# A router in four column groups: weights held still, tokens streamed, and the logits turned back

## The chip, the cores and the metric

The kernel runs on one core of a Trainium2 chip. The metric is the device time of one execution in microseconds (us); runs of the same kernel are given as a median with lowest and highest. The profile names the engines of the core: PE is TensorE (matrix products, PEld its weight loads), DVE is VectorE, ACT is ScalarE, POOL is GpSimd, SP is SyncE, which issues most DMA transfers. Each engine executes its own queue in order and waits on semaphores for the others.

## The reference

One macaron block: half a feed-forward step, attention, half a feed-forward step. Each takes a layer norm of x and is added to x. X is 16 x 256 x 256 float32, so 4096 tokens of 256 features. Cut to what matters here:

```python
# feed-forward (twice, with the same weights)
x = w_norm * xf * rsqrt(mean(xf * xf) + EPS)
logits = x @ w_router                       # 256 -> 32 experts
probs = softmax(logits)
w_topk, sel = top_k(probs, 4)               # each expert takes up to 128 tokens
y = (silu(buf @ w_gate) * (buf @ w_up)) @ w_down        # 32 experts, 176 wide
out = scatter of y, weighted with w_topk
sh = silu(x @ sw_gate) * (x @ sw_up) @ sw_down          # shared expert, 704 wide
out = out + sigmoid(x @ w_shared_gate) * sh             # the shared gate: one column
return inp + out
# attention: 16 heads, 8 key/value heads of 32, rope, tanh soft cap, causal softmax
```

All products of the kernel are in float32.

## The kernel before

The 4096 tokens are 32 tiles of 128, in eight groups (`g`) of four tiles. The x tile stays on chip for the whole kernel.

*Routing.* `route(n, g)` is a generator that makes the router of group g in feed-forward n (0 or 1). It emits a stretch of instructions and yields, and its caller emits other work between the stretches; the number that it yields is not used by the caller. Its stretches: moments (L220, L221) and roots; `xr`, the normalised tokens (L248); two halves of four transposes `pt` (L257), each turned into `xnT` by ScalarE (L260), with the update of x (L268) between; then the router. Eight matmuls write `pl` (L276): the stationary operand is a 128x128 piece of `xnT` (128 features by 128 tokens), the moving one is `wr`, 33 columns wide (32 experts and the shared gate), and two pieces of 128 features add up. VectorE copies `pl` to `lg` (L280), takes the gate column (L281), the maximum (L283) and the difference (L285). After the next yield come exp on ScalarE (L287) and the tail: sum, reciprocal, probabilities `pr` (L290 to L297), a copy of them into `xr` on POOL (L298), the write of `xr` to the table `xtab` in device memory (L299), the four largest of each token (L303 to L306) and `mask` (L307).

*Experts.* `slots` counts the mask with `pc` (L323), in four column groups of 32, and makes the lists of tokens `idx`; `expert` gathers 128 tokens (L413), turns them (`pte`, L429; `xgT`, L432), multiplies (`pge`, L437; `poe`, L450), scales the product to `y` (L452) and adds it to the sums `acc` in device memory with a scatter (L453). The 32 experts are pipelined three deep.

*The shared expert* is the filling. `shared(pool, g)` yields after each piece: five pieces of four matmuls `pg` (L390) and one of two, then four of six matmuls `po` (L402), whose result VectorE adds to x (L406). `Fill.take(us)` emits pieces until their named costs add up to `us`; what is taken too much is kept in `left` and makes the next take smaller. The pieces of group g may be taken when `ready` is above g.

*Order.* The order on TensorE is that of the program everywhere (`manual_schedule`), on VectorE, ScalarE and POOL in the attention only; elsewhere a planner with its own costs sets it. `feed_forward` calls route, slots and expert with takes between (the constants on top: ROUTE_FILL, MASK_FILL, EXPERT_FILL). The routing of groups 0 to 6 of the second feed-forward is spread over the attention's loop over `units`: a group's `route` starts in step j=1 of its turn and ends two turns later. In that loop `project` makes queries, keys and values (`pq` L503, `pv` L531), `scores` makes `sc` (L552) with tanh and exp on ScalarE, and `values` makes `den` and `y` (L598) in four column groups. When no group is left to project (`mine` is None, the last turns), those pieces are absent.

*Buffers.* The pool `ps1` has two PSUM buffers of the kind "mm", which `pt`, `pl`, `po`, `pc`, `pte`, `pq` and `pv` take in turn: a tile waits until the one before the last has been read.

*The end.* After the last scatter SP reads `acc` back in eight pieces; POOL (L465, and L745 for single tiles) and VectorE (L745) add them to x, and the groups are stored. Groups whose filling was finished when the experts ended are added and stored whole.

Of the kernel before, what the change touches and what calls it, by code (L numbers as in the profile page):

```python
# [22 lines left out]
GT = 4  # L23
# [17 lines left out]

ROUTE_FILL, SLOT_FILL, FIRST_FILL, EXPERT_FILL, SUM_FILL, PROJECT_FILL = 3.0, 1.7, 6.0, 2.4, 17.0, 1.5
LAST_FILL = 8.0
MASK_FILL, ROW_FILL = 4.0, 3.2
WARM = (9, 3)
AHEAD = 3
SPARE = (1.0, 0.0, 3.0, 4.0)
PROJECT_PIECES = ((2, 1), (0, 2), (2, 1), (0, 0))  # L50


_COLS = {}
_n = 0
for _name, _w in [("ident", P), ("cos", T), ("sin", T), ("triu", P), ("iota", CAP),
                  ("ustrict", P), ("last", P), ("block", P // NT), ("slot", 1), ("spare", 1), ("base", 1)]:
    _COLS[_name] = (_n, _w)
    _n += _w
# [3 lines left out]
def _constants():  # L62
    k = np.zeros((P, NCONST), np.float32)

    def put(name, value):
        o, w = _COLS[name]
        k[: value.shape[0], o : o + w] = value

    put("ident", np.eye(P))
    inv = (1.0 / np.float32(10000.0) ** (np.arange(0, HD, 2).astype(np.float32) / np.float32(HD))).astype(np.float32)  # L70
    freqs = np.arange(T, dtype=np.float32)[:, None] * inv[None, :]
    emb = np.concatenate([freqs, freqs], -1)
    put("cos", np.tile(np.cos(emb).T, (P // HD, 1)))

    sign = np.where(np.arange(HD) < HD // 2, -1.0, 1.0)
    put("sin", np.tile(np.sin(emb).T * sign[:, None], (P // HD, 1)))
    put("triu", np.triu(np.ones((P, P))))

    put("iota", np.tile(np.arange(CAP) + 0.5, (P, 1)))

    p = np.arange(P)[:, None]
    blocks = np.kron(np.eye(P // NT), np.ones((NT, NT)))
    put("ustrict", blocks * np.triu(np.ones((P, P)), 1))
    put("last", np.tile(p % NT == NT - 1, (1, P)))
    put("block", p // NT == np.arange(P // NT))
    put("slot", p + 0.5)
    put("spare", p + NTOK - P)
    put("base", p % NT * P)
    return k
# [3 lines left out]
def macaron_kernel(ctx: ExitStack, tc: tile.TileContext, X, Wq, Wk, Wv, Wo, w_norm, w_router, w_gate, w_up,  # L93
# [26 lines left out]
    def const(name, parts=P):  # L120
        o, w = _COLS[name]
        return kc[:parts, o : o + w]
# [8 lines left out]
    nc.gpsimd.memset(power, -0.5)  # L131
    wnorm = cpool.tile([P, 2], F32, name="wnorm")
    nc.sync.dma_start(wnorm, w_norm.rearrange("(c p) -> p c", p=P))
    wr = cpool.tile([P, 2, E + 1], F32, name="wr")
    nc.sync.dma_start(wr[:, :, 0:E], w_router.rearrange("(c p) e -> p c e", p=P))
    nc.sync.dma_start(wr[:, :, E : E + 1], w_shared_gate.rearrange("(c p) e -> p c e", p=P))


    sw = cpool.tile([P, 2, 2 * FS], F32, name="sw")
# [12 lines left out]
        load_x(g)  # L152
    nc.sync.dma_start(kc[:, P:], consts[:, P:])
    triu = cpool.tile([P, P], BF16, name="triu")
    nc.vector.tensor_copy(triu, const("triu"))

    wq = cpool.tile([P, 2, 2, 2, P], F32, name="wq")
    wk = cpool.tile([P, 2, C], F32, name="wk")
# [72 lines left out]
    def route(n, g):  # L231


        mv = moments(g)


        s2 = root("s2", mv, 1.0 + RMS_EPS, RMS_EPS * LN_EPS)
        s1 = root("s1", mv, 1.0, LN_EPS)
        xa = stat.tile([P, GT], F32, name="xa", bufs=5)
        nc.gpsimd.tensor_scalar(xa, s1, 0.5, 1.0, ALU.mult, ALU.add)  # L240
        xb = stat.tile([P, GT], F32, name="xb", bufs=5)
        nc.gpsimd.tensor_mul(xb, s1, mv[:, :, 0])
        nc.gpsimd.tensor_scalar_mul(xb, xb, -0.5)
        yield 0.0
        xr = rows.tile([P, GT, XW], F32, name="xr")
        for t in range(GT):
            i = g * GT + t
            nc.vector.tensor_scalar(  # L248
                xr[:, t, 0:C], x[:, i, :], mv[:, t, 0:1], s2[:, t : t + 1], ALU.subtract, ALU.mult
            )  # L250
        yield 0.0
        for h in range(GT // 2):
            pt = ps1.tile([P, 2, 2, P], F32, tag="mm", name="pt")
            for j in range(2):
                t = 2 * h + j
                for c in range(2):
                    nc.tensor.transpose(pt[:, c, j, :], xr[:, t, c * P : (c + 1) * P], ident)  # L257
            i0 = (g * GT + 2 * h) * P
            for c in range(2):
                nc.scalar.activation(  # L260
                    xnT[:, c, i0 : i0 + 2 * P], pt[:, c].rearrange("p j t -> p (j t)"), AF.Identity,
                    scale=wnorm[:, c : c + 1],
                )
            yield 0.5
            if h == 0:
                for t in range(GT):
                    i = g * GT + t
                    nc.scalar.activation(  # L268
                        x[:, i, :], x[:, i, :], AF.Identity, bias=xb[:, t : t + 1], scale=xa[:, t : t + 1]
                    )  # L270
                yield 0.0
        pl = ps1.tile([P, GT, E + 1], F32, tag="mm", name="pl")
        for t in range(GT):
            i = g * GT + t
            for c in range(2):
                nc.tensor.matmul(  # L276
                    pl[:, t, :], lhsT=xnT[:, c, i * P : (i + 1) * P], rhs=wr[:, c, :], start=(c == 0), stop=(c == 1)
                )
        lg = stat.tile([P, GT, E + 1], F32, name="lg", bufs=2)
        nc.vector.tensor_copy(lg, pl)  # L280
        nc.vector.tensor_copy(gate[:, g * GT : (g + 1) * GT], lg[:, :, E])  # L281
        mx = stat.tile([P, GT, 1], F32, name="mx")
        nc.vector.tensor_reduce(mx[:, :, 0], lg[:, :, 0:E], AX.X, ALU.max)  # L283
        ex = stat.tile([P, GT, E], F32, name="ex", bufs=2)
        nc.vector.tensor_sub(ex, lg[:, :, 0:E], mx.to_broadcast([P, GT, E]))  # L285
        yield 1.9
        nc.scalar.activation(ex, ex, AF.Exp)  # L287
        yield 0.0
        tot = stat.tile([P, GT, 1], F32, name="tot")
        nc.vector.tensor_reduce(tot[:, :, 0], ex, AX.X, ALU.add)  # L290
        nc.vector.reciprocal(tot, tot)

        pr = stat.tile([P, GT, E + 4], F32, name="pr", bufs=1)
        nc.vector.memset(pr[:, :, E : E + 4], -1.0)
        nc.vector.tensor_mul(ex, ex, tot.to_broadcast([P, GT, E]))

        nc.vector.scalar_tensor_tensor(pr[:, :, 0:E], ex, TINY, ex, ALU.is_ge, ALU.mult)  # L297
        nc.gpsimd.tensor_copy(xr[:, :, C:XW], pr[:, :, 0:E])  # L298
        nc.sync.dma_start(xtab[n][g * GW : (g + 1) * GW, :].rearrange("(t p) c -> p t c", p=P), xr)  # L299
        top = stat.tile([P, GT, 8], F32, name="top")  # L300
        hit = stat.tile([P, GT, E + 4], F32, name="hit", bufs=1)
        for t in range(GT):
            nc.vector.max(top[:, t, :], pr[:, t, 0:E])  # L303
        nc.vector.memset(top[:, :, TOPK:8], -1.0)
        for t in range(GT):
            nc.vector.match_replace(hit[:, t, :], top[:, t, :], pr[:, t, :], 2.0)  # L306
        nc.vector.tensor_single_scalar(  # L307
            mask[:, :, g * GT : (g + 1) * GT], hit[:, :, 0:E].rearrange("p t e -> p e t"), 1.5, ALU.is_gt
        )
        yield 0.0  # L310
# [61 lines left out]

    def shared(pool, g, last):

        sg = stat.tile([P, GT], F32, name="sg")
        nc.scalar.activation(sg, gate[:, g * GT : (g + 1) * GT], AF.Tanh, scale=0.5)
        nc.vector.tensor_scalar(sg, sg, 1.0, 0.125, ALU.add, ALU.mult)
        act = pool.tile([P, len(FC), GW], F32, name="act")
        cols = slice(g * GW, (g + 1) * GW)
        for k, (f0, fw) in enumerate(FC):  # L380
            pg = big.tile([P, 2, GW], F32, tag="big", name="pg")
            if fw == P:
                at = [f0, FC[-1][0] + f0]
                b = pg[:, 1, :]
            else:
                at = [2 * f0]
                b = pg[fw : 2 * fw, 0, :]
            for s, w0 in enumerate(at):
                for c in range(2):
                    nc.tensor.matmul(  # L390
                        pg[:, s, :], lhsT=sw[:, c, w0 : w0 + P], rhs=xnT[:, c, cols], start=(c == 0), stop=(c == 1)
                    )
            si = act[:fw, k, :]
            nc.scalar.activation(act[:, k, :], pg[:, 0, :], AF.Tanh, scale=0.5)  # L394
            nc.vector.scalar_tensor_tensor(si, si, 1.0, pg[:fw, 0, :], ALU.add, ALU.mult)  # L395
            nc.vector.tensor_mul(si, si, b)  # L396
            yield 1.7 * len(at)
# [260 lines left out]
    def feed_forward(n, pool, works, fill):  # L658


        for g, work in works.items():
# [7 lines left out]
            if n == 0 and g == 0:  # L669
                warm(WARM[1])  # L670
            fill.take(ROUTE_FILL)
            advance(work, 2)
            advance(later[2])
            fill.ready = g + 1
            fill.take(ROUTE_FILL)
            next(work)
        if n == 0:
# [74 lines left out]
    with tc.tile_pool(name="attn", bufs=1, reuse_waits="tile") as pool:  # L752
# [5 lines left out]
        for k in range(len(units) + 2):  # L758
# [37 lines left out]

            if j == 3:
                advance(routing.get(g - 1))
            spare_time(SPARE[j])
            if j == 3:  # L800
                advance(routing.get(g - 2))
# [63 lines left out]
```

## Time and profile before

| | us |
|---|---|
| median of 3 runs (lowest to highest) | 1070.91 (1069.13 to 1072.49) |
| the profiled execution: its time | 1070.05 |
| the profiled execution: its span | 1068.3 |
| TensorE busy in the span | 1031.8 |
| first route stage | 0 to 114 |
| slots and experts of the first feed-forward | 114 to 339 |
| attention, with the routing of groups 0 to 6 | 397 to 780 |
| slots and experts of the second feed-forward | 800 to 1038 |

The span is that of the instructions; the time of the execution has 1.7 us around it. A row of a group gives its line, engine, operation, the tiles (out<-in), shapes and count, then busy us and the mean ns of one, then the idle time of the engine before it and what ended that. A row of a timeline gives start, length and the same names, with the wait in brackets. A row of stages gives for each stretch the busy us of each engine, the clock that TensorE was granted (1.00 is full), the share of the DMA engines and GB/s. A matmul's length is its latency; several overlap, so their cost is read from the distance between starts.

### The profile page before, as it was taken

Reading aid. Unit: us, or ns where it says so; the run is one execution under the profiler, and the core shown is the slowest. Engines: PE = TensorE matmul, PEld = TensorE weight load, DVE = VectorE, ACT = ScalarE, POOL = GpSimd, SP = SyncE. Lnnn points to the kernel's source line nnn. Section 1 sums busy time; section 2 is a strip of 40 time slices with the busy share of each in tenths; the row PEclk is TensorE's granted clock in tenths of the full one; section 3 lists DMA queues with packets and bytes.
Section 4 is the critical chain, followed back from the end, with each engine's and each line's share of the span. In section 5 each row is a group of like instructions: output and inputs, shape, how many; then the busy total and the mean of one; then the engine's idle time right before and its main releaser. Section 6 shows DMA issues by size and latency. Waiting matters only on the chain.

```text
span 1068.3 us, 15597 instructions
## 1 busy us (share of the span) xinstructions
PE 1031.8 (97%) x5432; PEld 650.7 (61%) x5432; DVE 628.8 (59%) x1681; ACT 399.9 (37%) x761; POOL 499.3 (47%) x552
## 2 busy tenths in 40 slices
PE   9999999999999899999999999998999999999998
PEld 5657656777767544545455556554466567767675
DVE  5755664445343457777778777774556744443434
ACT  3343111222221246675658475756621112221210
POOL 4500102555542298788476767562311024545536
PEclk9999999999999999999999999999999999999999
DMA  9811701778773000000101010000030027777739
GB/s 297 243 69 45 233 12 48 170 159 172 168 164 58 30 21 1 20 21 2 42 1 42 2 43 1 23 1 23 25 82 23 6 56 157 163 153 170 167 55 314
DMA packets 137869, 92.97 MB, mean 87 GB/s; under 512 B 80512, under 2 KB 135104, under 8 KB 137792
## 3 DMA queue, kind: packets, MB, share of 16 engines
q1 hardware_dynamic: 125504, 74.16, 24.9%
q0 software_dynamic: 12288, 17.83, 9.7%
q8 instruction: 43, 0.70, 0.3%
q14 instruction: 34, 0.28, 0.1%
HBM read 60.99 MB, written 30.97 MB: 86 GB/s over the span
## 4 chain that ended last, share of the span: by engine, by line
PE 89%; DVE 6%; ACT 3%; issue 1%; DMA 0%; SPq 0%; POOL 0%; ACTq 0%; POOLq 0%
PE pg L390 28%; PE po L402 14%; PE pge L437 8%; PE pq L503 8%; PE poa L616 5%; PE poe L450 5%; PE sc L552 5%; PE y L598 3%; PE den L598 3%; PE pv L531 3%; PE pl L276 2%; PE pte L429 1%; PE pt L257 1%; DVE act L395 1%; DVE act L396 1%
## 5 line engine op out<-in xcount | busy, mean ns | idle before, releaser
L390 PE MATMUL pg<-xnT,sw 128*128 128x512 f32 x704 | 320.7, 600 | 1.8 <-ACT p L559 1.8
L390 PEld LDWEIGHTS pg<-xnT,sw 128*128 128x128 f32 x704 | 131.1, 192 | 138.8 <-issue 130.7
L453 POOL DMA_INDIRECT acc<-y,idx x64 | 101.4, 1584 | 183.6 <-DVE y L452 104.8
L402 PE MATMUL po<-swd,act 128*128 128x256 f32 x768 | 179.9, 383 | 6.6 <-DVE act L396 2.4
L402 PEld LDWEIGHTS po<-swd,act 128*128 128x128 f32 x768 | 143.0, 190 | 35.7 <-issue 13.0
L395 DVE SCALAR_TENSOR_TENSOR act<-act,pg 128x512 f32<-128x512 f32 x96 | 65.7, 684 | 167.9 <-ACT act L394 167.8
L394 ACT ACTIVATE act<-pg 128x512 f32<-128x512 f32 x96 | 57.2, 596 | 271.3 <-PE pg L390 271.3
L559 ACT ACTIVATE p<-sc 128x512 f32<-128x512 f32 (+1 forms) x128 | 97.4, 808 | 106.8 <-PE sc L552 106.3
L564 POOL TENSOR_SCALAR_AFFINE_SELECT p<-p 128x512 f32<-128x512 f32 x128 | 82.3, 667 | 48.1 <-ACT p L562 45.7
L413 POOL DMA_INDIRECT xg<-xtab,idx x64 | 67.9, 1061 | 76.8 <-DVE idx L368 57.9
L437 PE MATMUL pge<-xgT,wgu 128*112 128x128 f32 (+1 forms) x768 | 95.8, 275 | 5.9 <-issue 4.4
L562 ACT ACTIVATE p<-p 128x512 f32<-128x512 f32 (+1 forms) x128 | 100.9, 844 | 0.0
L437 PEld LDWEIGHTS pge<-xgT,wgu 128*112 128x112 f32 (+1 forms) x768 | 88.8, 182 | 8.7 <-issue 7.6
L552 PE MATMUL sc<-qT,kT 32*128 32x256 f32 (+1 forms) x512 | 68.5, 535 | 4.7 <-DVE act L396 3.4
L406 DVE SCALAR_TENSOR_TENSOR x<-po,sg,x 128x256 f32<-128x256 f32 x64 | 30.8, 483 | 69.2 <-PE po L402 68.9
L396 DVE TENSOR_TENSOR act<-act,pg 128x512 f32<-128x512 f32 x96 | 65.7, 685 | 2.4
L511 POOL TENSOR_TENSOR qs<-qs,kc 128x512 f32<-128x512 f32 x48 | 61.2, 1275 | 12.7 <-DVE qs L506 12.7
L432 ACT ACTIVATE xgT<-pte,wnorm 128x128 f32<-128x128 f32 x128 | 39.8, 364 | 71.3 <-PE pte L429 71.3
L450 PE MATMUL poe<-wd,sie 112*128 112x256 f32 x256 | 66.0, 380 | 0.1
L616 PE MATMUL poa<-wo,yT 128*128 128x256 f32 x256 | 59.8, 386 | 2.1 <-DVE qT L510 1.2
L503 PE MATMUL pq<-hT,wq 128*128 128x512 f32 x128 | 60.9, 600 | 0.0
L616 PEld LDWEIGHTS poa<-wo,yT 128*128 128x128 f32 x256 | 47.3, 190 | 19.8 <-ACT xnT L260 5.0
(110 smaller groups left out, 1343.7 us busy)
## 6 DMA issues: line engine op xcount, KB each, us to landing
xtab<-xr SPq DMA_DIRECT2D x16, 576.0 KB
acc<-zero SPq DMA_DIRECT2D x2, 4224.0 KB
a<-acc SPq DMA_DIRECT2D x16, 512.0 KB
wgu<-in_L_ffn_w_gate SPq DMA_DIRECT2D x64, 112.0 KB
wgu<-in_L_ffn_w_up SPq DMA_DIRECT2D x64, 112.0 KB
wd<-in_L_ffn_w_down SPq DMA_DIRECT2D x64, 112.0 KB
wgu<-in_L_ffn_w_gate SPq DMA_DIRECT2D x64, 64.0 KB
wgu<-in_L_ffn_w_up SPq DMA_DIRECT2D x64, 64.0 KB
```

What stands on the lines that cost most here:

```text
L390: nc.tensor.matmul(pg[:, s, :], lhsT=sw[:, c, w0 : w0 + P], rhs=xnT[:, c, cols], start=(c == 0), stop=(c == 1))
L395: nc.vector.scalar_tensor_tensor(si, si, 1.0, pg[:fw, 0, :], ALU.add, ALU.mult)
L402: nc.tensor.matmul(po, lhsT=act[:, k, t * P : (t + 1) * P], rhs=swd[:, k, :], start=(k == 0), stop=(k == len(FC) - 1),)
L437: nc.tensor.matmul(pg[:fw, n_, :], lhsT=wgu[:, c, w0 : w0 + fw], rhs=xgT[:, c, :], start=(c == 0), stop=(c == 1))
L450: nc.tensor.matmul(po, lhsT=si[:, k, :], rhs=wd[:, k, :], start=(k == 0), stop=(k == 1))
L453: nc.gpsimd.indirect_dma_start(out=acc[n], out_offset=bass.IndirectOffsetOnAxis(ap=idx[:, e : e + 1], axis=0), in_=y, in_offset=None, boun ...
L503: nc.tensor.matmul(pq, lhsT=weights[:, c, :], rhs=hT[:, c, :], start=(c == 0), stop=(c == 1))
L552: nc.tensor.matmul(sc[i // 2][:, i % 2, 0 : 2 * w].rearrange("p (s t) -> p s t", s=2), lhsT=kT[r, m, t0 + k0 : t0 + k0 + P], rhs=qT[r, m, ...
L559: nc.scalar.activation(parts[h], sc[h][:, :, 0 : 2 * w], AF.Tanh, scale=QK_SCALE / SOFTCAP)
L562: nc.scalar.activation(parts[h], parts[h], AF.Exp, scale=SOFTCAP)
L564: nc.gpsimd.affine_select(out=diag, in_=diag, compare_op=ALU.is_ge, fill=0.0, base=0, pattern=[[0, 4], [1, P]], channel_multiplier=-1,)
L616: nc.tensor.matmul(po, lhsT=yT[:, c // 2, c % 2, qh * P : (qh + 1) * P], rhs=wo[:, c // 2, c % 2, :], start=(c == 0), stop=(c == 3),)
```

## The change

The roles of the router's operands are exchanged. Now 32 columns of `wr` are stationary, and 128 tokens of `xnT` are moving. The four tiles of a group write to four column groups, partitions 32t to 32t+31 of `plt`. The shared gate no longer is a 33rd column: `wr` has a second set of 32 columns, of which the first is the gate and the rest are zeros (a memset on POOL), so there are 16 matmuls where eight were. ScalarE copies `plt` to `lt`; after a new yield two transposes bring both sets back to tokens on partitions as `pl`, from which gate, maximum and difference are read directly (the copy `lg` is gone).

Around it: the first ROUTE_FILL is 2.0 instead of 3.0, and a new take, LOGIT_FILL = 2.5, stands between the two stretches of the router, in `feed_forward` and, where nothing is projected, in the attention's loop; the filling of a group is released before that take. The shared expert's `sg` (tanh of the gate) is emitted ahead of its fourth piece instead of its first. The constant `triu` is made on VectorE from `iota` instead of loaded.

```diff
-ROUTE_FILL, SLOT_FILL, FIRST_FILL, EXPERT_FILL, SUM_FILL, PROJECT_FILL = 3.0, 1.7, 6.0, 2.4, 17.0, 1.5
+ROUTE_FILL, SLOT_FILL, FIRST_FILL, EXPERT_FILL, SUM_FILL, PROJECT_FILL = 2.0, 1.7, 6.0, 2.4, 17.0, 1.5
+LOGIT_FILL = 2.5
...
-    wr = cpool.tile([P, 2, E + 1], F32, name="wr")
-    nc.sync.dma_start(wr[:, :, 0:E], w_router.rearrange("(c p) e -> p c e", p=P))
-    nc.sync.dma_start(wr[:, :, E : E + 1], w_shared_gate.rearrange("(c p) e -> p c e", p=P))
+    wr = cpool.tile([P, 2, 2, E], F32, name="wr")
+    nc.gpsimd.memset(wr[:, 1], 0.0)
+    nc.sync.dma_start(wr[:, 0], w_router.rearrange("(c p) e -> p c e", p=P))
+    nc.sync.dma_start(wr[:, 1, :, 0:1], w_shared_gate.rearrange("(c p) e -> p c e", p=P))
...
-    nc.vector.tensor_copy(triu, const("triu"))
+    nc.vector.tensor_single_scalar(triu, const("iota"), slot, ALU.is_ge)
...
-        pl = ps1.tile([P, GT, E + 1], F32, tag="mm", name="pl")
-        for t in range(GT):
-            i = g * GT + t
+        plt = ps1.tile([P, 2, P], F32, tag="mm", name="plt")
+        for s in range(2):
             for c in range(2):
-                nc.tensor.matmul(
-                    pl[:, t, :], lhsT=xnT[:, c, i * P : (i + 1) * P], rhs=wr[:, c, :], start=(c == 0), stop=(c == 1)
-                )
-        lg = stat.tile([P, GT, E + 1], F32, name="lg", bufs=2)
-        nc.vector.tensor_copy(lg, pl)
-        nc.vector.tensor_copy(gate[:, g * GT : (g + 1) * GT], lg[:, :, E])
+                for t in range(GT):
+                    i = g * GT + t
+                    nc.tensor.matmul(
+                        plt[E * t : E * (t + 1), s, :], lhsT=wr[:, s, c, :], rhs=xnT[:, c, i * P : (i + 1) * P],
+                        start=(c == 0), stop=(c == 1),
+                    )
+        lt = stat.tile([P, 2, P], F32, name="lt", bufs=1)
+        nc.scalar.copy(lt, plt)
+        yield 1.2
+        pl = ps1.tile([P, 2, GT, E], F32, tag="mm", name="pl")
+        for s in range(2):
+            nc.tensor.transpose(pl[:, s].rearrange("p t e -> p (t e)"), lt[:, s, :], ident)
+        nc.vector.tensor_copy(gate[:, g * GT : (g + 1) * GT], pl[:, 1, :, 0])
...
-        nc.vector.tensor_reduce(mx[:, :, 0], lg[:, :, 0:E], AX.X, ALU.max)
+        nc.vector.tensor_reduce(mx[:, :, 0], pl[:, 0], AX.X, ALU.max)
...
-        nc.vector.tensor_sub(ex, lg[:, :, 0:E], mx.to_broadcast([P, GT, E]))
-        yield 1.9
+        nc.vector.tensor_sub(ex, pl[:, 0], mx.to_broadcast([P, GT, E]))
+        yield 0.2
...
-        sg = stat.tile([P, GT], F32, name="sg")
-        nc.scalar.activation(sg, gate[:, g * GT : (g + 1) * GT], AF.Tanh, scale=0.5)
-        nc.vector.tensor_scalar(sg, sg, 1.0, 0.125, ALU.add, ALU.mult)
...
+            if k == 3:
+                sg = stat.tile([P, GT], F32, name="sg")
+                nc.scalar.activation(sg, gate[:, g * GT : (g + 1) * GT], AF.Tanh, scale=0.5)
+                nc.vector.tensor_scalar(sg, sg, 1.0, 0.125, ALU.add, ALU.mult)
...
             fill.take(ROUTE_FILL)
+            next(work)
+            fill.ready = g + 1
+            fill.take(LOGIT_FILL)
             advance(work, 2)
             advance(later[2])
-            fill.ready = g + 1
             fill.take(ROUTE_FILL)
...
             if j == 3:
                 advance(routing.get(g - 1))
+            if j == 1:
+                advance(routing.get(g - 2))
+                if mine is None:
+                    spare_time(LOGIT_FILL)
             spare_time(SPARE[j])
```

## The prediction

> **What bounds the kernel now.** I read the page first: how busy each engine is, and the chain that ended last.
>
> ```profile
> PE 1031.8 (97%) x5432; PEld 650.7 (61%) x5432; DVE 628.8 (59%) x1681; ACT 399.9 (37%) x761; POOL 499.3 (47%) x552
> ...
> PE 89%; DVE 6%; ACT 3%; issue 1%; DMA 0%; SPq 0%; POOL 0%; ACTq 0%; POOLq 0%
> ```
>
> TensorE is the bound nearly everywhere, so a microsecond taken off its queue counts unless something else waits there. Second, the groups by shape, for what the change removes and for the nearest relatives of what it adds.
>
> ```profile
> L598 PE MATMUL y<-p,v 128*32 128x512 f32 x256 | 34.2, 606 | 0.0
> ...
> L276 PEld LDWEIGHTS pl<-wr,xnT 128*128 128x128 f32 x256 | 31.5, 194 | 5.2 <-issue 3.0 <-ACT xnT L260 1.6
> ...
> L276 PE MATMUL pl<-wr,xnT 128*128 128x33 f32 x256 | 30.9, 275 | 0.9 <-ACT xnT L260 0.7
> ...
> L257 PE MATMUL pt<-kc,xr 128*128 128x128 f32 x128 | 20.4, 283 | 2.5 <-DVE xr L248 2.5
> ...
> L280 DVE COPY lg<-pl 128x132 f32<-128x132 f32 x16 | 4.5, 281 | 15.0 <-PE pl L276 15.0
> ...
> L327 ACT COPY cum<-pc 128x256 f32<-128x256 f32 x8 | 2.6, 381 | 0.0
> ```
>
> An f32 matmul is two passes (8 matmuls in each of 16 groups, 256 records); a transpose is one. The mean of one record is its latency. What it costs is the distance to the next start, so third the timeline of TensorE alone, at a full-array router block and at the attention's products in four column groups (L598).
>
> ```profile
> 105.44 1.87 PE L276 MATMUL pl<-wr,xnT 128*128 128x33 f32 x16
> 107.14 7.11 PE L390 MATMUL pg<-xnT,sw 128*128 128x512 f32 x16
> ```
>
> ```profile
> 432.24 1.47 PE L598 MATMUL y<-p,v 128*32 128x512 f32 x16
> 433.53 0.61 PE L598 MATMUL den<-plate,ones 128*32 128x256 f32 x8
> 434.07 1.98 PE L503 MATMUL pq<-hT,wq 128*128 128x512 f32 x4
> ```
>
> Router: 16 passes in 1.70 us, some 0.11 each, although only 33 columns stream[...]. Column groups: y's 8 passes of 512 columns and 8 of 256 take 1.29. Full-array passes cost 0.429 for 512 (L390) and 0.216 for 256 (L402), so one after another they would take 5.16: four run at once.
>
> Fourth, the end of the span, as stages (us, PE, PEld, DVE, ACT, POOL, clock, DMA share, GB/s) and as a timeline.
>
> ```profile
> 1044.00:1050.00 6.00, 6.00 (x16) 2.66 (x15) 2.73 (x4) 1.19 (x2) 3.79 (x2) 1.00 1.07 356
> 1050.00:1056.00 6.00, 5.94 (x21) 3.64 (x20) 2.75 (x5) 1.19 (x2) 6.00 (x4) 1.00 1.09 348
> 1056.00:1062.00 6.00, 6.00 (x29) 5.28 (x29) 4.58 (x6) 0.00 (x0) 6.00 (x5) 1.00 1.09 385
> 1062.00:1067.00 5.00, 1.74 (x9) 1.19 (x7) 1.06 (x3) 0.00 (x0) 1.41 (x2) 1.00 1.04 365
> ```
>
> ```profile
> 1038.28 1.56 POOL L453 DMA_INDIRECT acc<-y,idx  x1 [2.90 <-issue]
> ...
> 1042.00 7.27 SPq L461 DMA_DIRECT2D a<-acc  x8
> ```
>
> From 1044 to 1067 the DMA engines are full: the sums are read back and the output is written. That began when the last scatter landed. So the end has two holders: TensorE (last pass 1063.8), and the last scatter (issued 1038.28) plus 30.0 us.
>
> **The change part by part.** (1) *TensorE per group.* Removed: 1.70. Added: 16 matmuls, 32 passes, in 8 rounds of four column groups. A 128-column full-array pass is 0.108 (transposes start 0.109 apart), so 0.86; and two transposes, 0.22. Together 1.08.
>
> Two rules of the Trainium skill speak against it. "TensorE: Matmul & The Clock Gate", in the section on 56 against 53.3 ns, gives a floor of some 25 ns between starts, but 62 ns per matmul if the sequencer issues them in microcode. By 62 ns the 32 passes take 2.0 us and each group loses 0.5. The row: in L598 the four starts of a round lie 7 ns apart, and the bf16 rounds of L323 (128 columns) follow each other after 46 to 57 ns for four. I take the row, 0.86. "TensorEngine Tiling (Array Packing)", Key Properties, says a change of tiling mode drains the array, without a price. This trace has one: den to pq (full array) is 0.309 between starts where den to den is 0.216, and pg to pc 0.523 where pg to pg is 0.429: 0.094 a switch. Without the rule 16 x (1.70 - 1.08) = 9.9. With it, 0.19 off at the ten groups with full-array neighbours (all eight of the first feed-forward, the last two of the second); in the attention plt follows L598 in the same mode and adds none. 9.9 - 1.9 = **8.0 us**.
>
> (2) *The round trip through ScalarE.* plt, then the copy lt (0.38 by L327), then pl. Nearest row for such a trip: pte to xgT to pge, where TensorE stands 0.57. In the first feed-forward a shared step (3.43, eight pg passes, or 2.59, twelve po passes) lies between, in five attention groups the pv block (3.45): hidden. For groups 5, 6 and 7 of the second the program order has pl right behind plt. At group 5 ScalarE's tanh limits what follows, so its 0.62 is lost; the other two cost 0.6 each: **-1.8**. But in group 6 only two po blocks follow instead of three, and a 1.5 wait there (po for VectorE's add, at 785) should go: +1.5.
>
> (3) *First route stage (0 to 114 us).* At the start pl's first half ran while xnT's second half was made; plt needs all four tiles in its first round. It starts near 12.5, at half clock: pg begins at 14.35 instead of 13.97, and group 0 gains nothing: -0.8. Then the largest wait of this stage:
>
> ```profile
> 60.93 1.12 PE L257 MATMUL pt<-kc,xr 128*128 128x128 f32 x4 [2.52 <-DVE xr L248]
> 61.84 4.83 PE L390 MATMUL pg<-xnT,sw 128*128 128x512 f32 x8
> ```
>
> pt waits for xr of group 4, which VectorE does behind the whole route tail of group 3, and the next pg block runs 1.2 long at half clock. In the new VectorE order xr comes ahead of max, match and mask: +3.9 at most, and I take it, since its DMA (xtab of group 2, issued 46.8) lands by 55. Other waits on po move about: +0.5. New: group 5's plt stands right behind its pt, so TensorE waits for xnT (ScalarE act 0.60, then 0.47): -1.2; po waits of groups 6 and 7: -0.8. Between the last pl and pc two pg blocks (6.87) shrink to one (3.43), while lg to mask took 4.3 (54.94 to 59.22), or 5.7 with an act pair between; behind pc stand all later passes: 1.0 to 2.4, taken 1.7. Sum **-0.1**.
>
> (4) *At no cost:* triu from iota (DVE, 0.19 as before); the memset of wr (POOL, under 0.4, done before SP reaches that DMA at 3.3); 64 KB less of constants; no lg copy on VectorE (16 x 0.28 = 4.5 us, idle 41%); 16 copies more on ScalarE (6 us, idle 63%); sg later. If VectorE were the cover's limit, (3) would change, not this.
>
> (5) *The filling moves.* SP's and POOL's queues keep their order but for two places. On TensorE, after the last poe stood po x6, pg x22, po x24; now pg x18, po x24. So 2.59 + 8 x 0.429 = **6.0 us** of shared-expert work now stand ahead of the last expert. The scatters make that matter: from the seventh expert of the second stage on, each starts 3.5 to 5 us behind its y, for the one before has to land; issues lie 4.5 to 5.3 apart.
>
> *Sum.* TensorE saves 8.0 - 1.8 + 1.5 - 0.1 = 7.6 ahead of the second expert stage. For expert 4 there one po block (2.6) has moved ahead: 5.0 sooner. For expert 8, two pg blocks (6.9): 0.7 sooner, plus 2.7 for the part of its 3.5 lag above the usual 0.8: the chain starts 3.4 sooner. I take 4.0 for the last scatter, nearer the later one. Its 30.0 us stay, as 4.2 MB in and 4.2 MB out are unchanged. The profiled execution took 1070.05 (span 1068.3 and 1.7 around it): 1066.05. The median is 0.86 above it: 1070.91 - 4.0 = **1066.9**.
>
> **The rivals.** *A: TensorE alone sets the end.* For: the chain that ended last is TensorE to within 5 us of the end. Against: the DMA share of the tail. Then 7.6 go through: 1063.3. *B: the waits eat it.* If the pt wait stays (3.9) and the mask wait takes its upper end (0.7 more), 3.0 are left, which the filling moved ahead of expert 8 takes back: 1070.5. *C, slower: ScalarE's queue in the attention.* Orders there are fixed, and lt may stand behind two tanh and two exp of the scores (2 x 0.60 + 2 x 0.63 = 2.5). pv's second tile needs plt's buffer 1.73 after plt. From that point on every us late is a us on five groups; at 2.0 late, 10 us: saving -2.4, expert 8 later by 6.9 + 2.4 - 2.7 = 6.6: 1077.5. For: ScalarE 63% busy there; against: those scores are issued 2 us before plt.
>
> **How the numbers follow.** Mine 0.50 (own range 1064.5 to 1069), A 0.20, B 0.15, C 0.15. A change under 0.3% (3.2 us, 1067.7 to 1074.1) can't be told from none. Faster: 0.36 of mine and 0.19 of A, 0.55; slower: most of C, 0.02 of B, 0.16; the rest 0.29. Range 1061 (A with its errors) to 1075.5 (between B and C).
>
> **What would show it.** plt's 32 passes in about 0.86, pl's two in 0.22; no 2.5 wait at pt near 58; a new wait of 1 to 2 at pc; in the attention no wait on lt. The last scatter near 1034, and 30 us from it to the end: if that distance is shorter, A was right. Passes 60 ns apart, or pv waiting for lt, would prove me wrong.

## The result and the profile after

| kernel | median us | lowest to highest | ratio to the kernel before |
|---|---|---|---|
| before | 1069.47 | 1066.58 to 1072.71 | |
| changed | 1076.66 | 1072.21 to 1078.67 | 1.0056, 95% interval 1.0045 to 1.0067 |

The change made the kernel 0.56% slower, some 6 us by the ratio, where 4.0 us of gain were forecast. The profiled execution has a span of 1074.9 us (before: 1068.3). The page of the changed kernel, the row of the engines and the chain that ended last:

```profile
PE 1029.9 (96%) x5720; PEld 638.8 (59%) x5720; DVE 626.9 (58%) x1665; ACT 405.9 (38%) x777; POOL 497.7 (46%) x550
...
PE 82%; DVE 10%; ACT 3%; DMA 2%; issue 1%; SPq 1%; POOL 1%; ACTq 0%; POOLq 0%; DVEq 0%
```

TensorE is busy 1.9 us less, in a span that is 6.6 us longer, and its share of the last chain fell from 89% to 82%: it waits. The router itself did what was forecast. Timeline of TensorE in the first route stage of the changed kernel (the first two rows are plt and pl of group 1, the plt at 37.11 and the pl at 45.09 are those of group 2):

```profile
26.22 1.08 PE L281 MATMUL plt<-xnT,wr 128*32 128x128 f32 x32
...
30.77 0.38 PE L290 MATMUL pl<-kc,lt 128*128 128x128 f32 x2
...
37.11 1.08 PE L281 MATMUL plt<-xnT,wr 128*32 128x128 f32 x32
38.12 2.43 PE L413 MATMUL po<-swd,act 128*128 128x256 f32 x10
44.11 1.19 PE L413 MATMUL po<-swd,act 128*128 128x256 f32 x2 [3.57 <-DVE act L407]
45.09 0.63 PE L290 MATMUL pl<-kc,lt 128*128 128x128 f32 x2
45.88 5.07 PE L413 MATMUL po<-swd,act 128*128 128x256 f32 x12 [0.15 <-DVE x L417]
...
58.81 0.38 PE L290 MATMUL pl<-kc,lt 128*128 128x128 f32 x2
59.03 3.60 PE L401 MATMUL pg<-xnT,sw 128*128 128x512 f32 x8
```

plt takes 1.01 us from start to start between full-array neighbours, pl 0.22. But between plt and pl of group 2 TensorE stops for 3.6 us, at 40 to 44, and the twelve po passes behind the stop take 5.07 us instead of 2.86. Before the change the stop at that place was 1.2:

```profile
43.06 0.67 PE L402 MATMUL po<-swd,act 128*128 128x256 f32 x2 [1.21 <-DVE ex L285]
```

The stretches of the changed kernel (TensorE's busy us, granted clock, DMA share, GB/s) say why:

```profile
40.00:44.00 4.00, 0.55 (x3) 0.95 0.98 299
44.00:48.00 4.00, 3.74 (x9) 0.50 1.04 349
48.00:51.00 3.00, 3.00 (x10) 0.60 1.04 349
```

The clock fell to half after the stop (0.50, then 0.60). What the stop waits for stands on VectorE and in SP's queue (timelines of the changed kernel):

```profile
38.98 0.66 DVE L406 SCALAR_TENSOR_TENSOR act<-act,pg 64x512 f32<-64x512 f32 x1
41.75 1.38 DVE L251 TENSOR_SCALAR xr<-x,mv,s 128x256 f32<-128x256 f32 x4 [2.12 <-DMA xtab<-xr]
43.16 0.69 DVE L407 TENSOR_TENSOR act<-act,pg 64x512 f32<-64x512 f32 x1
```

```profile
38.54 0.37 SPq L309 DMA_DIRECT2D xtab<-xr  x1
```

`xr` has two buffers, so group 3's waits until group 1's has been written out. That DMA is issued at 38.54 (before: 35.09). The pl of group 1 now stands one step of filling later, but that alone does not explain 3.5 us: the probabilities pr are only 0.7 us later. The rest comes on POOL, which copies them into xr (VectorE and POOL; the kernel before, then the changed one):

```profile
34.42 0.29 DVE L297 SCALAR_TENSOR_TENSOR pr<-ex 128x128 f32<-128x128 f32 x1
34.77 0.29 POOL L298 COPY xr<-pr 128x128 f32<-128x128 f32 x1 [1.18 <-DVE pr L297]
```

```profile
35.15 0.28 DVE L307 SCALAR_TENSOR_TENSOR pr<-ex 128x128 f32<-128x128 f32 x1
35.84 2.02 POOL L231 TENSOR_TENSOR s<-s,power 128x4 f32<-128x4 f32 x2
38.23 0.29 POOL L308 COPY xr<-pr 128x128 f32<-128x128 f32 x1
```

Before, POOL waited for pr and copied it at once. Now the planner has put the roots of a later group (s) ahead of the copy, which starts 2.8 us after pr is ready. The shared expert's last act stands behind xr on VectorE, and po behind act.

In the attention a second effect appears, at five groups alike (TensorE, changed kernel):

```profile
594.21 1.06 PE L281 MATMUL plt<-xnT,wr 128*32 128x128 f32 x32
595.19 3.72 PE L542 MATMUL pv<-wv,hT 128*128 128x256 f32 x16
598.75 0.38 PE L290 MATMUL pl<-kc,lt 128*128 128x128 f32 x2
...
600.13 1.99 PE L514 MATMUL pq<-hT,wk 128*128 128x512 f32 x4
602.49 1.95 PE L514 MATMUL pq<-hT,wq 128*128 128x512 f32 x4 [0.37 <-DVE ex L295]
```

plt and pl take 0.98 + 0.31 where the old router took 1.79, and pv does not wait for lt. But two pq now start 2.36 apart instead of 1.82: the second needs pl's PSUM buffer, and VectorE reads pl (at 601.69 to 602.3) only behind the next group's moments. From the first den to pg (592.03 to 607.31 here) the group takes 15.28 us, before and after.

The end (scatters on POOL, then VectorE, then TensorE, changed kernel):

```profile
1038.68 1.56 POOL L464 DMA_INDIRECT acc<-y,idx  x1 [2.84 <-DVE y L463]
1043.17 1.56 POOL L464 DMA_INDIRECT acc<-y,idx  x1 [2.93 <-DVE act L407]
```

```profile
1055.77 0.48 DVE L417 SCALAR_TENSOR_TENSOR x<-po,sg,x 128x256 f32<-128x256 f32 x1 [0.85 <-PE po L413]
1062.66 2.53 DVE L758 TENSOR_TENSOR x<-x,a 128x256 f32<-128x256 f32 x1 [6.41 <-DMA a<-acc]
1065.11 0.47 DVE L417 SCALAR_TENSOR_TENSOR x<-po,sg,x 128x256 f32<-128x256 f32 x1
```

```profile
1052.67 8.23 PE L413 MATMUL po<-swd,act 128*128 128x256 f32 x36
1065.64 5.48 PE L413 MATMUL po<-swd,act 128*128 128x256 f32 x12 [4.73 <-DVE x L417]
```

The last scatter is issued 4.9 us later than before (1038.28). VectorE waits 6.41 for the sums read back, po cannot be taken from PSUM meanwhile, TensorE stops for 4.73 and does its last twelve passes at a clock of 0.52 to 0.63.

So the theory taken to the experiments had three causes: (a) the stop in the first route stage, (b) pl's buffer in the attention, (c) the shared expert's work, of which 6.0 us more stand ahead of the last expert. The rivals: the new form of the router costs by its trip through ScalarE, or TensorE alone sets the end and it is harmless where the filling is cut.

### The profile page after: what moved, and what is told of

Same layout as the page of the kernel before. It is cut to its first block, busy times and chain, and to the rows that moved or that the text cites. A ratio compares the mean times of both kernels' runs of the same rounds, so it can differ in the third digit from the quotient of the medians.

```text
span 1074.9 us, 16193 instructions
## 1 busy us (share of the span) xinstructions
PE 1029.9 (96%) x5720; PEld 638.8 (59%) x5720; DVE 626.9 (58%) x1665; ACT 405.9 (38%) x777; POOL 497.7 (46%) x550
## 4 chain that ended last, share of the span: by engine, by line
PE 82%; DVE 10%; ACT 3%; DMA 2%; issue 1%; SPq 1%; POOL 1%; ACTq 0%; POOLq 0%; DVEq 0%
PE pg L401 25%; PE po L413 14%; PE pge L448 8%; PE pq L514 6%; PE poa L627 5%; PE poe L461 5%; PE sc L563 4%; PE y L609 3%; PE den L609 3%; PE pv L542 3%; DVE st L223 2%; DVE act L406 1%; DVE act L407 1%; PE pte L440 1%; PE plt L281 1%
## 5 line engine op out<-in xcount | busy, mean ns | idle before, releaser
L413 PE MATMUL po<-swd,act 128*128 128x256 f32 x768 | 185.1, 391 | 12.9 <-DVE act L407 6.7
L413 PEld LDWEIGHTS po<-swd,act 128*128 128x128 f32 x768 | 146.2, 194 | 43.1 <-issue 14.6
L308 POOL COPY xr<-pr 128x128 f32<-128x128 f32 x16 | 4.8, 297 | 117.0 <-DVE pr L307 105.7
```

What stands on the lines that cost most here:

```text
L413: nc.tensor.matmul(po, lhsT=act[:, k, t * P : (t + 1) * P], rhs=swd[:, k, :], start=(k == 0), stop=(k == len(FC) - 1),)
```

## The experiments

All ratios are to runs of the kernel before in the same comparison (medians 1070.1 to 1070.8 us). In the edits, "feed_forward" is the function of that name.

**The tail.** Run e3 is the changed kernel with the second stage's experts cut as before the change:

```diff
-        fill.take(FIRST_FILL)
+        fill.take(FIRST_FILL if n == 0 else 1.0)
```

> The changed kernel with 5 us less filling asked for ahead of the first expert of the second feed-forward: the shared-expert work is then cut at the second stage's experts exactly as before the change (31.8 us of it are left behind the last poe instead of 25.8). Theory: the 6.0 us of filling moved ahead of the last expert delay its scatter, from which a nearly fixed 30 us run to the end; put back, the last scatter comes 4 to 6 us sooner than 1043.2, the wait of 4.7 us for x in the last po blocks goes with it, and the end comes 5 to 7 us below the changed kernel: ratio 0.999 to 1.001. Rival (TensorE alone sets the end, the sum of its work is the same): the end moves by less than 1.5 us, ratio 1.0045 or more.

1070.90 us, ratio 1.0004 (0.9990 to 1.0019): by the ratios 0.0052, or 5.6 us, below the changed kernel, as theory (c) said. Its last scatter:

```profile
1038.30 1.56 POOL L464 DMA_INDIRECT acc<-y,idx  x1 [3.03 <-issue]
```

Run e6 does the reverse, the kernel before with only `11` in place of FIRST_FILL's 6.0 in the second feed-forward:

> The kernel before with nothing changed but the cut of the shared expert's work in the second feed-forward: 5 us more are asked for ahead of its first expert, so that 25.8 us of it are left behind the last poe instead of 31.8, as in the changed kernel. Theory: the last scatter comes 5 to 6 us later than 1038.3, the end with it: 1075 to 1076, ratio 1.0045 to 1.006. Rival (TensorE alone sets the end): its sum of work is unchanged, the end moves by less than 1.5 us, ratio below 1.0015.

1076.52 us, ratio 1.0046 (1.0026 to 1.0066). The last scatter came 5.1 us later than 1038.28:

```profile
1043.35 1.56 POOL L453 DMA_INDIRECT acc<-y,idx  x1 [2.94 <-DVE act L396]
```

No other work was changed, so the cut of the filling alone costs 5 us, and "TensorE alone sets the end" is refuted. Run e4, the kernel before with all of the new placing and the old router:

```diff
...
             fill.take(ROUTE_FILL)
-            advance(work, 2)
+            next(work)
+            fill.ready = g + 1
+            fill.take(LOGIT_FILL)
+            next(work)
             advance(later[2])
-            fill.ready = g + 1
             fill.take(ROUTE_FILL)
...
+            if j == 1 and mine is None:
+                spare_time(LOGIT_FILL)
             spare_time(SPARE[j])
```

> The kernel before with only the new placing of the filling (the smaller fill ahead of each group's router, the new fill behind it, groups ready earlier, the new fill in the last attention groups); the router itself and the late sg are the old ones. Theory: the placing alone costs what the tail costs, 5 to 7 us, and saves nothing: ratio 1.005 to 1.0065, about that of the whole change; pl is not split, so the wait of xr for xtab of group 1 is absent or below 1 us. Rival (the new form of the router is what costs, by its round trip through ScalarE and its waits): the kernel stays within 2 us of the kernel before, ratio 0.999 to 1.002.

1075.19 us, ratio 1.0053 (1.0032 to 1.0075). It can't be told from the changed kernel: the placing alone can account for the loss, and whatever the new router saves does not show. The traces don't tell the two routers apart in the first route stage with this placing: pc began at 111.7 here and at 112.7 in the changed kernel, but the first pte at 180.88 and 180.21, and 1.7 us of e4's time up to there are one po block at half clock (4.54 instead of 2.86 us). The execution profiled was the fastest of six, 2.9 us below their median.

**The first route stage.** Run e1 gave xr a third buffer (in the first feed-forward), run e5 eight. The edit of e1:

```diff
-    def route(n, g):
+    def route(n, g, rows=rows):
...
-        first = {g: route(0, g) for g in range(NG)}
-        advance(first[0], 2)
-        feed_forward(0, pool, first, fill)
+        with tc.tile_pool(name="rows0", bufs=3) as rows0:
+            first = {g: route(0, g, rows0) for g in range(NG)}
+            advance(first[0], 2)
+            feed_forward(0, pool, first, fill)
```

> The changed kernel with three buffers instead of two for the normalised rows xr of the first feed-forward; nothing else is moved. Theory: in the first route stage VectorE's xr of group 3 waited 2.12 us for the DMA of group 1's xtab (issued 3.5 us later than before, because pl comes one step of filling later), act of the shared expert stands behind it in VectorE's order, TensorE waited 1.2 us for that and then ran twelve po passes in 5.07 us instead of 2.86. With the buffer free, the wait and the long passes go: pc of the first stage comes 3.0 to 3.5 us sooner than 112.7, and the end, if nothing takes it back, is 3 us below the changed kernel: ratio to the kernel before 1.0028. Rival (the later pl itself delays what TensorE needs, the buffer is only where the delay is seen): another wait of the same size takes its place, and the time stays within 1 us of the changed kernel, ratio 1.005 to 1.006.

> The changed kernel with one buffer for each group's xr in the first feed-forward (eight, where three only let the planner put the next group's xr at the same place, behind the same DMA). Theory: no xr waits for a DMA any more, the 2.1 us wait of VectorE ahead of the last act of group 0 goes, TensorE's 3.6 us stop at 40 to 44 us with it, and so do the twelve po passes at half clock: pc of the first stage starts near 109.5 instead of 112.7, and the end is 2.5 to 3.5 us below the changed kernel, ratio to the kernel before 1.0025 to 1.0035. Rival (the stop is made by the order and load of VectorE in this stage, of which the buffers are only one part): pc stays within 1 us of 112.7, ratio 1.005 or more.

Both missed. e1 took 1079.12 us, ratio 1.0081 (1.0058 to 1.0103), e5 1080.21 us, ratio 1.0102 (1.0074 to 1.0130); pc came at 115.5 and 116.0 instead of 112.7. VectorE and TensorE in e5:

```profile
36.24 0.73 DVE L251 TENSOR_SCALAR xr<-x,mv,s 128x256 f32<-128x256 f32 x2 [1.39 <-POOL s L231]
```

```profile
33.86 0.44 PE L290 MATMUL pl<-kc,lt 128*128 128x128 f32 x2 [2.66 <-ACT lt L286]
...
39.35 0.65 PE L260 MATMUL pt<-kc,xr 128*128 128x128 f32 x4 [1.18 <-ACT xnT L263]
```

Outside the attention the order on VectorE, ScalarE and POOL is the planner's. In e1 it put the next group's xr at the same spot, behind the same DMA (VectorE waited 2.12 there again). That DMA, xtab of group 1, was issued at 40.9 in e1 and at 41.9 in e5, later still than 38.5. In e5 no xr waited for a DMA any more, and VectorE waited for POOL's roots instead, ScalarE's lt and xnT came late, and TensorE waited for those. That the two buffers had also kept later groups' work out of the way is a reading of these orders, and was not tested apart. Run e8 gave the eight buffers to the kernel before:

> The kernel before with the eight buffers for xr in the first feed-forward and the old router. If the buffers help only because the new router's pl comes later, this kernel stays within 1 us of the kernel before, ratio 0.999 to 1.001, or gains the 2.5 us that pt waited near 58. If they help any router alike, it gains as much as the buffers gain on the changed kernel, 2.5 to 3.5 us, ratio 0.9965 to 0.998.

1072.05 us, ratio 1.0013 (1.0003 to 1.0022). The wait of 2.5 us at pt near 58 did go, but the stop at po grew from 1.2 to 2.6. Neither branch of the expectation: it is slightly slower. Buffers are no mend for either router.

The late pl itself was tested in run e12, the changed kernel with one edit, which puts group 1's pl right behind its plt:

```diff
             fill.ready = g + 1
-            fill.take(LOGIT_FILL)
+            early = n == 0 and g == 1
+            fill.take(0.0 if early else LOGIT_FILL)
             advance(work, 2)
             advance(later[2])
-            fill.take(ROUTE_FILL)
+            fill.take(ROUTE_FILL + (LOGIT_FILL if early else 0.0))
```

> The changed kernel with only the edit of the first route stage (group 1's pl right behind its plt, the filling that stood between them behind pl); attention and tail are left as changed. If what this edit gave beside the two other mends, 0.0029 of the time or 3.1 us, comes through without them too, the ratio to the kernel before is 1.0025 to 1.003, pc of the first stage starts near 109 instead of 112.7, and the last scatter comes 3 to 4 us sooner than 1043.2. If the tail holds the end whatever comes before it, the ratio stays at 1.0045 or more although pc comes sooner.

1070.68 us, ratio 1.0004 (0.9988 to 1.0019). pc began at 108.7, xtab of group 1 was issued at 36.13 and the last scatter at 1038.83. The probabilities of group 1 were ready at 35.3, hardly sooner than in the changed kernel (35.4), but their copy now stood ahead of the roots on POOL (VectorE and POOL in e12):

```profile
35.06 0.28 DVE L307 SCALAR_TENSOR_TENSOR pr<-ex 128x128 f32<-128x128 f32 x1
35.82 0.29 POOL L308 COPY xr<-pr 128x128 f32<-128x128 f32 x1
```

So the edit works through the order that the planner gives to POOL; no run moved the copy alone. The first-stage gain of 4.0 us was as expected, but by the ratios 5.6 us of time came through, not 3.1. The end shows where more came from: VectorE waited 3.19 us for the sums instead of 6.41, and TensorE 0.35 instead of 4.73, at full clock.

```profile
1050.38 8.23 PE L413 MATMUL po<-swd,act 128*128 128x256 f32 x36
1058.97 2.86 PE L413 MATMUL po<-swd,act 128*128 128x256 f32 x12 [0.35 <-DVE x L417]
```

From the last pass of poe to the last pass of all TensorE needs 26.7 us here and 33.5 in the changed kernel, with the same work. So the stop at the end is not linear: it goes when the scatters come early enough, by whatever edit. Two single mends share it, and their gains don't add up. One thing stays open: in the two profiled executions the last poe came 2.3 us sooner, the last scatter 4.3, and why the chain of scatters gained the other 2.0 was not traced.

Run e11 puts pl right behind plt at all groups of the first feed-forward and places its filling as before the change (with the mends of tail and attention, see e9):

```diff
...
+            if n == 0:
+                fill.take(3.0)
+                advance(work, 3)
+                advance(later[2])
+                fill.ready = g + 1
+                fill.take(3.0)
+                next(work)
+                continue
```

> The same two mends, and in the first feed-forward the placing of the filling of the kernel before, with pl right behind plt at all eight groups: the new router alone in the old stage. Its TensorE work is 8 x 0.43 us less than the old router's, and eight bare trips through ScalarE cost 0.57 each, 4.6 us: with the same filling ahead of it, pc of the first stage starts near 115.4 where the kernel before has 114.2, and the ratio is 0.0005 to 0.0015 above that of the run with the two mends alone. If the trips cost more than that, or the wait of 2.5 us at pt near 58 comes back unchanged, pc is at 117 or later. If pc comes before 114, the new placing of the filling in this stage, and not the router, was what cost.

1071.64 us, ratio 1.0003 (0.9989 to 1.0018), so within the interval of e9 below. But pc came at 120.9, not near 115.4. A bare trip cost TensorE 0.55 us at five groups, as expected, and 0.92 at one, but 4.6 at group 0 and 2.8 at group 2, as on ScalarE lt stood behind updates of x that waited for POOL (group 0):

```profile
17.42 0.60 ACT L271 ACTIVATE x<-x,xb,xa 128x256 f32<-128x256 f32 x1 [4.60 <-POOL xb L246]
17.93 0.35 ACT L286 COPY lt<-plt 128x256 f32<-128x256 f32 x1
```

The fill between plt and pl thus saves some 0.6 us at most groups, more where ScalarE is held up, and it did harm at group 1.

**The attention.** Run e2 exchanges two lines in the attention's loop, so that VectorE reads pl ahead of the moments:

```diff
+                advance(routing.get(g - 2))
                 routing[g - 1] = route(1, g - 1)
                 next(routing[g - 1])
-                advance(routing.get(g - 2))
```

> The changed kernel with one exchange in the attention: pl and VectorE's three reads of it stand ahead of the next group's moments, not behind them. Theory: pl's PSUM buffer is held until those reads are done, at 602.3, and the second pq of the block needs it: TensorE stands some 0.54 us at each of five groups. With the exchange the two pq start 1.8 apart instead of 2.36, den to pg falls from 15.28 to 14.7 us per group, and the end comes 2.7 us below the changed kernel: ratio to the kernel before 1.003. Rival 1 (pq waits for the ScalarE or VectorE work behind an earlier pq, not for pl's buffer): the 0.54 stay, ratio 1.0056. Rival 2 (the scatters' chain sets the end): the last poe comes 2.7 sooner and the end does not, ratio 1.005 or more.

1075.26 us, ratio 1.0045 (1.0029 to 1.0061). The wait at pq went, as the timeline of TensorE in e2 shows:

```profile
598.69 1.98 PE L514 MATMUL pq<-hT,wk 128*128 128x512 f32 x4
600.51 1.88 PE L514 MATMUL pq<-hT,wq 128*128 128x512 f32 x4
```

Each of the five groups became 0.61 us shorter, 3.05 in all. Of that, the profiled execution gave back 2.4 by the end of the attention: 0.6 at a po block that waits for VectorE's act (the wait rose from 0.45 to 1.05 near 611), 0.2 at the next, and 1.6 around one block of poa (the attention's output product, at 760), which took 5.2 us instead of 3.7 after a drop of the clock. The mechanism is shown; of its gain about 1 us remains, and the interval does not exclude none.

**Together.** Run e7 had e2, e3 and e5's buffers, e9 only e2 and e3, e10 those two and the edit of e12.

> The changed kernel with the three mends together: eight buffers for xr, pl's reads ahead of the moments in the attention, and the shared expert's work cut at the second stage's experts as before the change. Theory: the three add up, 3 (first route stage) + 2.7 (attention) + 6 (tail) below the changed kernel: about 1065, ratio 0.994 to 0.997, and this is what the new router was worth. Rival (the gains end in the scatters' chain or in other waits): the kernel equals the kernel before within its interval, ratio 0.999 to 1.001.

> The changed kernel with two mends: pl's reads ahead of the moments in the attention, and the shared expert's work cut at the second stage's experts as before the change. The first route stage is left as changed. If the two earlier single runs add up (1.0004 with the tail, 0.0011 less by the order), the ratio to the kernel before is 0.999 to 0.9995; if the full 2.7 us of the five attention groups come through, 0.998. A ratio above 1.0004 would say that the order gives nothing once the tail is mended, because the scatters' chain holds the end.

> The run before with one edit in the first route stage: group 1's pl stands right behind its plt, and the filling that stood between them behind pl. Theory: the late pl of group 1 is what makes its xtab's DMA late, xr of group 3 waits for that, act and TensorE for xr. TensorE pays one bare trip through ScalarE, about 0.6 us, xtab of group 1 is issued near 35 instead of 38.5, the stop of 3.6 us at 40 to 44 us falls to 1.5 or less, and so do the po passes at half clock: pc of the first stage starts at 108.5 to 110.5 instead of 112.7, the end comes 2 to 3.5 us below the run before it, ratio 0.996 to 0.9975. Rival (VectorE and ScalarE have no more to give in this stage, whatever is placed where): pc stays within 1 us of 112.7, and the ratio within 0.001 of the run before.

| run | median us | ratio to the kernel before |
|---|---|---|
| e7: order, tail, eight buffers | 1073.34 | 1.0037 (1.0021 to 1.0052) |
| e9: order, tail | 1070.68 | 0.9995 (0.9983 to 1.0006) |
| e10: order, tail, early pl | 1067.85 | 0.9966 (0.9950 to 0.9982) |

e7 missed because of the buffers. e10 did what it was to do: xtab of group 1 was issued at 35.71, and TensorE's stop and half clock went (timeline, then stretches, of e10):

```profile
42.40 0.67 PE L413 MATMUL po<-swd,act 128*128 128x256 f32 x2 [1.31 <-DVE cum L338]
42.91 0.38 PE L290 MATMUL pl<-kc,lt 128*128 128x128 f32 x2
43.65 2.86 PE L413 MATMUL po<-swd,act 128*128 128x256 f32 x12 [0.36 <-DVE x L417]
```

```profile
40.00:44.00 4.00, 2.33 (x12) 1.00 1.02 342
44.00:48.00 4.00, 3.73 (x21) 1.00 1.05 349
```

pc began at 108.3, the last scatter at 1034.5, and the end came 31.1 us later. This version is 0.34% faster than the kernel before, some 3.6 us, and 0.9% faster than the changed one. How much of the 3.6 us is the router's own was not measured: no run gave the old router this mended placing.

## Why the prediction was wrong

*Step (1), TensorE per group: right.* plt takes 0.98 to 1.01 with its switches, pl 0.22 to 0.31, against 0.86 + 0.22 + 0.19 at most. Once VectorE reads pl early (e2), each of the five attention groups is 0.61 shorter than before the change, forecast 0.62. The row (column groups start 7 ns apart) was the better guide; by the 62 ns that the prediction quotes, plt would take 2.0.

*Step (2), the trip through ScalarE: right where it was looked at.* At groups 5 to 7 of the second feed-forward TensorE waits 0.49, 0.49 and 0.55 for lt (forecast some 0.6 each), and the wait of 1.5 near 785 went. lt is hidden in five attention groups; rival C did not happen. But only TensorE's own wait for lt was priced, not how long pl's buffer is held: pl now stands behind pv, and VectorE's three reads of it behind the next group's moments. That cost 0.54 at each of five groups. The copy lg used to free the buffer with one read of 0.26; three reads take 0.65 (601.69 to 602.34), so its removal, priced at nothing in step (4), may be some 0.4 of the 0.54. That is an estimate from these rows: no run kept lg.

*Step (3), the first route stage: this is the step that failed.* By the first pte, with equal filling ahead of it, 3.3 us of gain were forecast (eight groups of 0.43, and -0.1); the changed kernel was 3.4 late (180.21 against 176.77). The forecast gain at pt near 58 came (no wait of 2.5 stands there), and the new wait at pc came (1.8, forecast 1.7). What was missed is the stop at 40 to 44: it is 2.4 longer than before, and the half clock behind it costs 2.7 more. xr of group 3, which the prediction had let start earlier for free, waits for the xtab DMA of group 1, which comes 3.5 us later than before. The prediction followed the new order on VectorE but not the one on POOL: with pl one step of filling later, pr was only 0.7 later, but its copy fell behind the roots of a later group. It checked the landing of group 2's transfer for group 4, not that of group 1's for group 3. Of the 6.7 us that were missing, run e12 recovers 4.0 by pc, after paying 0.55 for its bare trip, and about 1 more was waited at pa (a later product of the slots, near 160) than before; about 1 us stays untraced. Its term for the start was off too, without much effect: pg began at 13.53, not 14.35, but pl then waited 0.88 for lt.

*Step (5), the filling that moves: the mechanism right, its sum spoiled by step (3).* "The last scatter plus 30.0 us" held within 2 us: 30.0 before, 30.2 in e6, 31.1 in e3, e9 and e10, 31.7 in the changed kernel. The prediction's terms for the moved filling make the last scatter 4.2 later without any saving (6.9 less 2.7 of slack); e6 measured 5.1. But the TensorE saving that was to pay for it was 0.2 us at the last poe instead of 7.6: that poe starts 5.8 later, with 6.0 of filling more ahead of it. Of the 7.4 that are missing there, 6.7 were missing at the first pte already, from step (3). So the last scatter was 4.9 later instead of 4.0 sooner. The 1.7 that the distance grew were not foreseen, and their cause stays open. The distance is 30.0 to 30.2 in all four traces of the old router and 30.9 to 31.8 in all ten of the new one, with the stop of TensorE at the end (e6: a stop of 2.3, and 30.2) or without it (e3: none, and 31.1).

*The rivals.* B, the waits eat the gain, named the right kind of failure and the wrong place: it put the remaining wait at pt. Its sum does not follow the prediction's own way for expert 8 either: 3.0 less 6.9 plus 2.7 is 1.2 us of loss, 1072.1 and not 1070.5. C's 1077.5 lies nearest to the 1076.7 measured, but that is luck: its mechanism did not happen. The prediction counted half clock behind the old wait at pt; no case of it had a new stop of TensorE, nor the half clock behind one.

## What to carry to other kernels

Splitting a step in two with work between moves everything that hangs on its second half; follow it through the queue of every engine on the way (here 0.7 us became 3.5 behind other work on POOL) to the DMA that frees a buffer, and find who is queued behind the waiter. When a copy is removed, ask how long the PSUM buffer is now held and what stands ahead of the reads. Filling in front of the last link of a serial chain of transfers cost nearly its full length here (6.0 us ahead, 5.1 later in e6), and two edits that relieve the same stop don't add up.

## What was not expected of the hardware

How much clock a stop costs is not set by its length alone. The same stop of 2.0 us at pc (start to start; a wait of 1.8) was followed by full clock in the changed kernel and by 0.66 over the next 4 us in e3 (stretches of TensorE; the changed kernel first, then e3):

```profile
108.00:112.00 4.00, 2.91 (x7) 1.00 0.02 9
112.00:116.00 4.00, 3.27 (x15) 1.00 1.02 335
```

```profile
108.00:112.00 4.00, 2.27 (x6) 1.00 0.18 66
112.00:116.00 4.00, 3.92 (x14) 0.66 1.02 332
```

In e12 the eight pg passes behind the same stop took 5.40 us, as in e3, where the changed kernel needs 3.70. In e9 two waits of 1.1 us each were enough: the clock was 0.57 from 762 to 766, while the same two waits left it at 1.00 in e3. The Trainium skill, "TensorE: Matmul & The Clock Gate", in the section "What's actually happening", says that activity is watched in a free-running window of about 3.4 us, and that the clock falls after at least one such window of idleness. A dependence on where the stop falls agrees with the first, but was not shown; the second does not hold here, where waits of 1.1 and 1.8 us were enough. Each of these drops was worth 1.7 us, 0.16% of the kernel, so single profiled executions can differ by as much as the smaller effects under study. It was not tried to place a stop on purpose.
